# Selective scan: one scan per state group, in place, started from the last states, with a new order of a step

## The chip, the cores and the metric

The program runs on one core of one Trainium2 chip. The metric is device microseconds of one execution; below, "us" is microseconds. Engines are named as in the profile: PE (matrix products), DVE (vector), ACT (activations), POOL (the general engine), SP (issues nearly all DMAs).

## What is computed

Four layers, each added to its input `x` of 8 images of 64 x 64 positions and 96 channels, after a group norm: two selective scans (layers 0 and 2), a chunked scan (layer 1), and a layer that widens, squares and narrows the image (layer 3). The change touches layers 0 and 2 only. Each of these projects the input to 192 channels, runs a 3 x 3 convolution and a SiLU, reads the 4096 positions in four directions (rows, columns, and both backwards), and scans each direction with 16 states a channel. Cut to what matters:

```python
delta = jax.nn.softplus(delta + delta_bias[None, :, None])

def step(h, inp):
    ut, dt, bt, ct = inp
    dA = jnp.exp(dt[..., None] * A4)                  # 4 directions, 192 channels, 16 states
    dBu = (dt * ut)[..., None] * bt[:, :, None, :]
    h = h * dA + dBu
    y = jnp.einsum('bkdn,bkn->bkd', h, ct)
    return (h, y)
...
return y + u * D[None, :, None]
```

The four directions are then added up, normalised, gated and projected back. All is in fp32.

## The kernel before

`tile_vision_stack` loops over the 8 images and, for each, over the layers. `selective_scan` (called 16 times) works one layer. Its convolution comes first, partly on DVE and partly on PE. Then come 32 **steps**: four directions `k`, each in eight pieces `c` of 512 positions. Directions 2 and 3 are scanned from the end, with reversed views of the same tiles. A step has six **units** `n`, each 32 of the 192 channels. In a unit, partition 32 j + c holds state j of a group for channel c, so 16 states are four **groups** of four: a unit is a tile of 128 partitions and 4 x 512 elements.

The work of a unit `t` (counted over all steps) is spread over the engines:

- `spread` (L821): PE repeats delta times u of 32 channels over 128 partitions, to the PSUM tile `pu`. Its pool `p_misc` has one buffer.
- `with_b` (L828): the product of that with B, to the tile `db`. Units 2 and 5 run on POOL, with a copy `du2` that came through DRAM; the other four on DVE.
- `decays` (L840): ACT computes exp(A delta) in PSUM. There are two tiles `da`, each for two groups.
- `scan` (L854): DVE, h = h da + db along the row. One instruction covers two groups in one row of 1026. Each group has 513 places: the additional one holds a decay of zero and, in `db`, the state with which the group starts. `enter` (L811) copies these states on ACT from `states`, three units ahead.
- `leave` (L871): ACT keeps the last column of h as the state for the next piece; POOL multiplies h by C in place.
- `total_y` (L885): PE sums over the states of three units, on top of the `y` so far, into the PSUM tile `py`; ACT copies it to `y`. It is done twice a step, after units 2 and 5.

`prepare` (L720) is a generator that makes the inputs of a step, and `prepare_part` runs it on to its next `yield`: a projection on PE, its copy on ACT, a second projection, its copy with the DMAs that write B and C to DRAM and bring B back to 128 partitions, softplus on ACT (which changes the activation table and back), the DMAs of delta, those of `dx` for the first three units and of C, `du` = delta times u on POOL with its trip through DRAM, and last `dx` for the other three units. Both projections use `py`'s buffer (pool `p_y`, one buffer).

`Beside` (L619) runs the last layer of the image before, in pieces: `begin` issues a piece's matrix products, `end` its copy on ACT. Up to four pieces fall in a step. The first image has none.

What sets the order is the program: inside `tc.manual_schedule()` each engine, and SP as the queue of DMAs, works its instructions in the order in which the Python code issues them, and waits for semaphores where its inputs or buffers are not ready. The order is written in the loop over `t` near the end of `selective_scan`.

Of the kernel before, what the change touches and what calls it, by code (L numbers as in the profile page):

```python
# [9 lines left out]
F32 = mybir.dt.float32  # L10
AF = mybir.ActivationFunctionType
ALU = mybir.AluOpType
PSUM = bass.MemoryType.PSUM
# [9 lines left out]
LC = 512  # L23
NCH = L // LC
SEG = LC + 1
NCG = 6
NSG = 4
# [40 lines left out]
def tile_vision_stack(  # L68
# [20 lines left out]
    nc = tc.nc  # L89
# [24 lines left out]
    zero = wp.tile([128, NSG], F32, name="zero")  # L114
# [565 lines left out]
    def selective_scan(w, wdt, dgw, a, d, u, y, beside):  # L680
# [23 lines left out]
        with (  # L704
# [3 lines left out]
            tc.tile_pool(name="scan", bufs=3) as gp,  # L708
            tc.tile_pool(name="state", bufs=2) as stp,
            tc.tile_pool(name="beside", bufs=1) as bp,  # L710
            tc.tile_pool(name="p_misc", bufs=1, space=PSUM) as pmp,
            tc.tile_pool(name="p_y", bufs=1, space=PSUM) as pyp,
            tc.tile_pool(name="p_da", bufs=1, space=PSUM) as pap,
# [6 lines left out]
            def prepare(i):  # L720
# [10 lines left out]
                pv = pyp.tile([128, LC], F32, name="pv", tag="py")  # L731
# [9 lines left out]
                pv = pyp.tile([128, LC], F32, name="pv", tag="py")  # L741
# [50 lines left out]
                m["du"] = du  # L792
                dud = dp.tile([32, 2, LC], F32, name="dud")
                nc.sync.dma_start(dud, du[64:96])
                m["du2"] = du2 = tp.tile([128, 2, LC], F32, name="du2")
# [5 lines left out]
            def groups(t):  # L801

                return t[:, 1:].rearrange("p (g s) -> p g s", s=SEG)[:, :, :LC]

            def places(t, n, rev):

                return t[:, rev : n * SEG + rev].rearrange("p (g s) -> p g s", s=SEG)[
                    :, :, SEG - 1 if rev else 0
                ]

            def enter(t):  # L811

                i, n = t // units, t % units
                k, c = steps[i]
                first = c == (0 if k < 2 else NCH - 1)
                db = gp.tile([128, NSG * SEG + 1], F32, name="db")
                src = zero if first else states[i - 1][:, NSG * n : NSG * n + NSG]
                nc.scalar.copy(places(db, NSG, int(k >= 2)), src)
                made[i]["db", n] = db

            def spread(t):  # L821

                m, n = made[t // units], t % units
                rows = slice(32 * (n % 3), 32 * (n % 3) + 32)
                m["pu"] = pu = pmp.tile([128, LC], F32, name="pu", tag="misc")
                nc.tensor.matmul(pu, sel[rows, :], m["du"][rows, n // 3, :], start=True, stop=True)  # L826

            def with_b(t):  # L828

                m, n = made[t // units], t % units  # L830
                pool = n % 3 == 2
                (nc.gpsimd if pool else nc.vector).tensor_mul(  # L832
                    groups(m["db", n]),
                    (m["du2"][:, n // 3, :] if pool else m["pu"])
                    .unsqueeze(1)
                    .to_broadcast([128, NSG, LC]),
                    m["b"],
                )

            def decays(t, p):  # L840

                i, n = t // units, t % units
                k, _ = steps[i]
                dst = das[p][:, 1:].rearrange("p (g s) -> p g s", s=SEG)
                for g in range(2):
                    gs = 2 * p + g
                    nc.scalar.activation(  # L847
                        dst[:, g, :LC],
                        made[i]["dx"][n // 3][:, n % 3, :],
                        AF.Exp,  # L850
                        scale=av4[:, k, n, gs : gs + 1],
                    )

            def scan(t, p):  # L854
                i, n = t // units, t % units
                k, _ = steps[i]
                rev = int(k >= 2)
                way = slice(None, None, -1) if rev else slice(None)
                at = slice(2 * p * SEG + rev, 2 * (p + 1) * SEG + rev)
                if p == 0:  # L860
                    made[i]["h", n] = gp.tile([128, NSG * SEG + 1], F32, name="h", bufs=5)
                nc.vector.tensor_tensor_scan(  # L862
                    made[i]["h", n][:, at][:, way],
                    das[p][:, rev : 2 * SEG + rev][:, way],
                    made[i]["db", n][:, at][:, way],
                    0.0,
                    ALU.mult,
                    ALU.add,
                )

            def leave(t, more):  # L871

                i, n = t // units, t % units
                k, _ = steps[i]
                h = groups(made[i]["h", n])
                if n == 0:
                    states[i] = stp.tile([128, NCG * NSG], F32, name="state")
                nc.scalar.copy(  # L878
                    states[i][:, NSG * n : NSG * n + NSG], h[:, :, 0 if k >= 2 else LC - 1]
                )  # L880
                if more:
                    prepare_part(i + 1)
                nc.gpsimd.tensor_mul(h, h, made[i]["c"])  # L883

            def total_y(i, hf):  # L885
# [11 lines left out]
                hs = [groups(made[i].pop(("h", 3 * hf + q))) for q in range(3)]  # L897
# [14 lines left out]
            def prepare_part(i):  # L912
                if i < len(steps):
                    if i not in going:
                        going[i] = prepare(i)
                    next(going[i], None)
# [5 lines left out]
            das = [pap.tile([128, 2 * SEG + 1], F32, name=f"da{p}") for p in range(2)]  # L922
# [16 lines left out]
            for da in das:  # L939
                for at in range(3):  # L940
                    nc.vector.memset(da[:, at * SEG : at * SEG + 1], 0.0)
# [4 lines left out]
            for _ in range(2):  # L946
                prepare_part(0)
            conv_half(6, 0, pyp, "py")
            for t in range(3):
                enter(t)  # L950
            decays(0, 0)
            decays(0, 1)
# [12 lines left out]
            spread(0)  # L965
            for _ in range(3):
                prepare_part(1)
            conv(w, y, u, (40, 48), 0)
            with_b(0)
            other = Beside(ops)  # L970
            for t in range(total + 2):
                n, i = t % units, t // units
                ahead = t + 1 < total
                quota = (i + 1) * len(ops) // len(steps) - i * len(ops) // len(steps)
                if n == 2 and quota > 1:
                    other.begin(pyp, "py")
                if n in (0, 3) and ahead:
                    spread(t + 1)
                elif n == 1 and t + 2 < total:
                    spread(t + 2)  # L980
                if n == 0 and i > 0:
                    sums = total_y(i - 1, 1)
                elif n == 3:
                    sums = total_y(i, 0)
                elif n == 4:
                    if quota > 3:
                        other.begin(pmp, "misc")
                    if t + 2 < total:
                        spread(t + 2)
                    prepare_part(i + 2)  # L990
                elif n == 5:
                    prepare_part(i + 2)
                if t < total:
                    scan(t, 0)
                    if n % 3 == 0 and t + 2 < total:
                        with_b(t + 2)
                if ahead:
                    decays(t + 1, 0)
                if n == 1:
                    if t > 1:  # L1000
                        nc.scalar.copy(*sums)
                    if t < total:
                        other.begin(pyp, "py")
                elif n == 2:
                    other.end()
                    if quota > 2:
                        other.begin(pyp, "py")
                elif n == 3:
                    other.end()
                elif n == 4:  # L1010
                    nc.scalar.copy(*sums)  # L1011
                    other.end()
                if t < total:
                    scan(t, 1)
                    leave(t, n == 3)
                if t + 3 < total:
                    enter(t + 3)
                if ahead:
                    decays(t + 1, 1)
                    if (n + 1) % 3 != 2:  # L1020
                        with_b(t + 1)
                if n in (1, 2):
                    other.end()
                    if n == 2 and quota > 4:
                        other.begin(pyp, "py")
                if n in (4, 5):
                    prepare_part(i + 2)
                if n in (0, 1, 5):
                    prepare_part(i + 1)
# [815 lines left out]
```

## Time and profile before

| | us |
|---|---|
| median of three runs | 26687.65 (26685.59 to 26688.1) |
| the profiled execution | 26693.06 |
| its span, first to last instruction | 26691.2 |
| one selective scan, first to last scan instruction, first image | 1159.2, 1159.3 |
| the same, later images (fourteen) | 1186.3 to 1207.1, mean 1195.5 |
| all sixteen | 19055 |

The profile page gives the busy time of each engine, a row per group of equal instructions (line, engine, operation, output <- inputs, shapes, count; then busy us, mean ns of one; then the idle time of the engine before them, and what ended it), and the waits. "L862" is a line of the kernel. A timeline lists the instructions of an engine by start and length, with equal neighbours merged. Since neighbours on an engine may overlap a little, the price of an instruction in a row is read from start to start. The table's last three lines come from the first and last scan of each layer.

### The profile page before, as it was taken

Reading aid. Unit: us, or ns where it says so; the run is one execution under the profiler, and the core shown is the slowest. Engines: PE = TensorE matmul, PEld = TensorE weight load, DVE = VectorE, ACT = ScalarE, POOL = GpSimd, SP = SyncE. Lnnn points to the kernel's source line nnn. Section 1 sums busy time; section 2 is a strip of 40 time slices with the busy share of each in tenths; the row PEclk is TensorE's granted clock in tenths of the full one; section 3 lists DMA queues with packets and bytes.
Section 4 is the critical chain, followed back from the end, with each engine's and each line's share of the span. In section 5 each row is a group of like instructions: output and inputs, shape, how many; then the busy total and the mean of one; then the engine's idle time right before and its main releaser. Section 6 shows DMA issues by size and latency. Waiting matters only on the chain. (4 is left out here: it accounts for less than half of the span.)

```text
span 26691.2 us, 282273 instructions
## 1 busy us (share of the span) xinstructions
PE 21984.9 (82%) x90981; PEld 8484.0 (32%) x90981; DVE 23982.3 (90%) x16689; ACT 16407.9 (61%) x29921; POOL 21235.6 (80%) x7928
## 2 busy tenths in 40 slices
PE   6796788888888878888888887888888888788888
PEld 2151222422224222242223422234222342223424
DVE  9989999898998989889898898988989889898896
ACT  5656566565665656556565565655656556565564
POOL 8949898497975979759797697976979769796694
PEclk7787777877778777787778877788777887778878
DMA  5515454154541545425453254532545325453352
GB/s 125 122 35 129 120 129 109 41 132 123 131 107 47 131 123 132 102 50 133 123 132 97 58 132 123 133 90 62 132 123 132 85 68 133 123 133 78 75 132 68
DMA packets 1678115, 2836.59 MB, mean 106 GB/s; under 512 B 434473, under 2 KB 477769, under 8 KB 1672033
## 3 DMA queue, kind: packets, MB, share of 16 engines
q1 hardware_dynamic: 1660000, 2812.23, 43.3%
q8 instruction: 731, 11.98, 0.2%
q10 hardware_dynamic: 16640, 6.29, 0.1%
q14 instruction: 744, 6.09, 0.1%
HBM read 2390.02 MB, written 427.49 MB: 106 GB/s over the span
## 5 line engine op out<-in xcount | busy, mean ns | idle before, releaser
L862 DVE TENSOR_TENSOR_SCAN h<-da,db 128x1026 f32<-128x1026 f32 x6144 | 13745.7, 2281 | 744.8 <-ACT da L847 378.5
L883 POOL TENSOR_TENSOR h<-h,c 128x2048 f32<-128x2048 f32 x3072 | 12743.1, 4172 | 968.2 <-ACT state L878 528.3
L900 PE MATMUL py<-h,cst 128*32 128x512 f32 x24576 | 5344.6, 749 | 473.0 <-POOL h L883 472.6
L847 ACT ACTIVATE da<-dx,a0s 128x512 f32<-128x512 f32 x6144 | 4239.6, 690 | 1548.8 <-DVE h L862 1373.0
L847 ACT ACTIVATE da<-dx,a2s 128x512 f32<-128x512 f32 x6144 | 4239.2, 690 | 1546.5 <-DVE h L862 1375.0
L832 POOL TENSOR_TENSOR db<-du,b 128x2048 f32<-128x2048 f32 x1024 | 4661.3, 4552 | 306.7 <-DMA du<-dud 226.5
L832 DVE TENSOR_TENSOR db<-pu,b 128x2048 f32<-128x2048 f32 x2048 | 4643.3, 2267 | 141.6 <-PE pu L826 138.2
L826 PE MATMUL pu<-du,cst 32*128 32x512 f32 x4096 | 2940.8, 805 | 1455.7 <-DVE db L832 927.4
L900 PEld LDWEIGHTS py<-h,cst 128*32 128x32 f32 x24576 | 1217.5, 133 | 4997.2 <-issue 3829.7
L826 PEld LDWEIGHTS pu<-du,cst 32*128 32x128 f32 x4096 | 735.2, 223 | 3145.9 <-DVE db L832 1580.8
L743 PE MATMUL pv<-u,wk 96*128 96x512 f32 x2048 | 1290.5, 762 | 388.1 <-ACT raw L738 388.1
L506 PE MATMUL ps<-s,w3as 96*128 96x512 f32 x1344 | 1069.4, 888 | 641.7 <-ACT sf L513 258.9
L1349 ACT ACTIVATE sg<-sg 128x768 f32<-128x768 f32 x1024 | 819.6, 800 | 862.2 <-PE sg L1333 862.2
L890 PE MATMUL py<-y,cst 96*96 96x512 f32 x1536 | 1306.1, 946 | 9.0 <-ACT y L1011 5.7
L733 PE MATMUL pv<-u,wk 96*96 96x512 f32 x2048 | 1200.9, 716 | 59.6 <-DVE u L281 27.4
L1303 POOL TENSOR_TENSOR ce<-ec,cr 112x512 f32<-112x512 f32 x256 | 521.5, 2037 | 754.9 <-ACT ec L1301 736.6
L1381 DVE TENSOR_TENSOR wt<-wt,cbm 128x768 f32<-128x768 f32 x1024 | 990.6, 1001 | 128.9 <-ACT wt L1350 128.1
L878 ACT COPY state<-h 128x4 f32<-128x4 f32 x3072 | 588.6, 192 | 796.5 <-DVE h L862 788.2
L526 PE MATMUL ps<-w3bs,sf 128*128 128x96 f32 x5376 | 1071.5, 356 | 0.0
L314 POOL TENSOR_SCALAR xn<-xs,sb 96x512 f32<-96x512 f32 x192 | 204.8, 1069 | 997.9 <-PE pz L319 440.8
L526 PEld LDWEIGHTS ps<-w3bs,sf 128*128 128x128 f32 x5376 | 992.9, 270 | 0.0
L738 ACT COPY raw<-pv 96x512 f32<-96x512 f32 x512 | 297.6, 581 | 970.1 <-PE pv L733 943.5
(238 smaller groups left out, 29900.9 us busy)
## 6 DMA issues: line engine op xcount, KB each, us to landing
dx<-dd SPq DMA_DIRECT2D x4096, 192.0 KB
b<-bcd SPq DMA_DIRECT2D x2048, 256.0 KB
c<-bcd SPq DMA_DIRECT2D x2048, 256.0 KB
du<-dud SPq DMA_DIRECT2D x2048, 128.0 KB
dd<-raw SPq DMA_DIRECT2D x1024, 192.0 KB
dud<-du SPq DMA_DIRECT2D x512, 128.0 KB
xd<-xs SPq DMA_DIRECT2D x256, 192.0 KB
cr<-bcd SPq DMA_DIRECT2D x1536, 32.0 KB
```

The source lines that it names most:

```text
L506: nc.tensor.matmul(ps, w3as[:, m * 128 : (m + 1) * 128], live["x2"], start=True, stop=True)
L526: nc.tensor.matmul(po, live["f"][m][:, at : at + 128], w2q[:, m, :], start=False, stop=(m == 2),)
L733: nc.tensor.matmul(pv[:DM], weights[k][:, hi, 128:], uv[hi], start=(hi == 0), stop=(hi == 1))
L743: nc.tensor.matmul(pv, weights[k][:, hi, :128], uv[hi], start=(hi == 0), stop=(hi == 1))
L826: nc.tensor.matmul(pu, sel[rows, :], m["du"][rows, n // 3, :], start=True, stop=True)
L832: (nc.gpsimd if pool else nc.vector).tensor_mul(groups(m["db", n]), (m["du2"][:, n // 3, :] if pool else m["pu"]) .unsqueeze(1) .to_broadc ...
L847: nc.scalar.activation(dst[:, g, :LC], made[i]["dx"][n // 3][:, n % 3, :], AF.Exp, scale=av4[:, k, n, gs : gs + 1],)
L862: nc.vector.tensor_tensor_scan(made[i]["h", n][:, at][:, way], das[p][:, rev : 2 * SEG + rev][:, way], made[i]["db", n][:, at][:, way], 0. ...
L883: nc.gpsimd.tensor_mul(h, h, made[i]["c"])
L890: nc.tensor.matmul(py, skip[:, hf, :] if k == 0 else ident[:DM, :DM], near((u if k == 0 else y)[:, hf, :], wh, c * LC, LC), start=True, st ...
L900: nc.tensor.matmul(turn_back(py[32 * q : 32 * q + 32, :], wh, LC), red, cut(hs[q][:, g, :], wh), start=False, stop=(g == NSG - 1),)
L1381: nc.vector.tensor_mul(it["wt"], it["wt"], m["cbm"][:, j : j + 1, :].to_broadcast([128, RK, Q]),)
```

## The change

Nine edits, all in `selective_scan`:

- The scan works one group of 512 at a time, 24 instructions a step in place of 12. Its input and output are the same tile `h`: `with_b` writes there, and the scan overwrites it. The first value of a group is no place of the row any more but an operand, a column of `states` (or of `zero` at a direction's first piece).
- The additional places, `enter`, `groups`, `places` and the memsets of the separators are gone. The pool `scan` has 8 tiles `h` (before, 3 `db` and 5 `h`). `room` takes a unit's tile ahead of its writer, in the order of units.
- `da` is four PSUM tiles, one a group, and each is refilled right after its scan.
- `p_misc` has two buffers, so that two spreads can be ahead.
- A new PSUM pool `p_side` with one buffer serves the projections of `prepare` and the pieces of `Beside`, which leave `p_y` to `total_y`.
- `prepare` has two more `yield`s: the product `du`, its way to DRAM and its way back are three parts.
- The loop follows a table `plan`: for each unit, words issued ahead of the scans and after each of the four scans. `a`: room; `b`: product with B; `s`: spread; `p`: begin a piece; `e`: end it; `y`: sum of y; `c`: its copy; `r`: a part of `prepare`. The number is how many units (or steps, for `r`) ahead, and for `p` which piece of the step.
- The products with B on DVE stand between a unit's second and third scan, for the next unit (before: behind the unit's last scan, right ahead of the scan that reads them). On POOL, `du` now comes before the product with C of unit 2 (before: of unit 3).
- The sum of y of units 3 to 5 stands at the next step's start behind a spread and a piece, its copy in unit 2 (before: unit 1). That of units 0 to 2 stands in unit 4 (before: unit 3), its copy at the end of unit 5 (before: unit 4).

```diff
-            tc.tile_pool(name="scan", bufs=3) as gp,
+            tc.tile_pool(name="scan", bufs=8) as gp,
...
-            tc.tile_pool(name="p_misc", bufs=1, space=PSUM) as pmp,
+            tc.tile_pool(name="p_misc", bufs=2, space=PSUM) as pmp,
             tc.tile_pool(name="p_y", bufs=1, space=PSUM) as pyp,
+            tc.tile_pool(name="p_side", bufs=1, space=PSUM) as psp,
...
-                pv = pyp.tile([128, LC], F32, name="pv", tag="py")
+                pv = psp.tile([128, LC], F32, name="pv", tag="ps")
...
                 m["du"] = du
+                yield
                 dud = dp.tile([32, 2, LC], F32, name="dud")
                 nc.sync.dma_start(dud, du[64:96])
+                yield
                 m["du2"] = du2 = tp.tile([128, 2, LC], F32, name="du2")
...
-                m["pu"] = pu = pmp.tile([128, LC], F32, name="pu", tag="misc")
+                m["pu", n] = pu = pmp.tile([128, LC], F32, name="pu", tag="misc")
...
+            def room(t):
+
+                m, n = made[t // units], t % units
+                if ("h", n) not in m:
+                    m["h", n] = gp.tile([128, NSG, LC], F32, name="h")
+                return m["h", n]
...
+            def decay(t, g):
 
                 i, n = t // units, t % units
                 k, _ = steps[i]
+                nc.scalar.activation(
+                    das[g],
+                    made[i]["dx"][n // 3][:, n % 3, :],
+                    AF.Exp,
+                    scale=av4[:, k, n, g : g + 1],
+                )
+
+            def scan(t, g):
+                i, n = t // units, t % units
+                k, c = steps[i]
+                way = slice(None, None, -1) if k >= 2 else slice(None)
+                first = c == (0 if k < 2 else NCH - 1)
+                at = NSG * n + g
+                h = made[i]["h", n][:, g, :][:, way]
+                nc.vector.tensor_tensor_scan(
+                    h,
+                    das[g][:, way],
+                    h,
+                    zero[:, g : g + 1] if first else states[i - 1][:, at : at + 1],
+                    ALU.mult,
+                    ALU.add,
+                )
...
-            das = [pap.tile([128, 2 * SEG + 1], F32, name=f"da{p}") for p in range(2)]
+            das = [pap.tile([128, LC], F32, name=f"da{g}") for g in range(NSG)]
...
+            plan = (
+                ("a1 b2 s3 p1 y", "", "b1 s4", "", "e p2"),
+                ("", "", "", "", "r1 e p3"),
+                ("r1", "", "b1 c e p4", "", ""),
+                ("a1 b2 s3 s4", "e", "b1 r2", "", "r2"),
+                ("r1 y r2", "", "r1", "", ""),
+                ("r1", "", "b1", "", "c r2"),
+            )
...
+                for word in plan[n][0].split():
+                    act(word, t, quota)
+                for g in range(NSG):
+                    scan(t, g)
+                    if g == NSG - 1:
+                        leave(t, n == 2)
+                    if t + 1 < total:
+                        decay(t + 1, g)
+                    for word in plan[n][1 + g].split():
+                        act(word, t, quota)
+            nc.scalar.copy(*total_y(len(steps) - 1, 1))
```

`leave`'s second argument says that a part of `prepare` (the product `du`) goes on POOL's queue ahead of the unit's product with C.

## The prediction

> **What bounds the kernel now.** I read the page's busy shares first, then a table of windows, then the costliest groups, the waits, and last the timeline of one step, engine by engine. Here are the shares, and one window of 100 us in the first image's selective scan and one in the second's (columns: PE, PEld, DVE, ACT, POOL busy, granted clock, DMA share, GB/s).
>
> ```profile
> PE 21984.9 (82%) x90981; PEld 8484.0 (32%) x90981; DVE 23982.3 (90%) x16689; ACT 16407.9 (61%) x29921; POOL 21235.6 (80%) x7928
> ...
> 600.00:700.00 100.00, 70.16 (x176) 20.21 (x176) 98.15 (x45) 62.05 (x120) 100.00 (x26) 0.72 0.53 130
> 4000.00:4100.00 100.00, 82.93 (x234) 26.66 (x233) 95.27 (x44) 66.11 (x126) 96.27 (x25) 0.74 0.52 123
> ```
>
> In this stage DVE and POOL are both full: a gain on one alone ends at the other. From the second image on, the previous image's last layer runs beside the scan, and DVE falls to 95%. The groups:
>
> ```profile
> L862 DVE TENSOR_TENSOR_SCAN h<-da,db 128x1026 f32<-128x1026 f32 x6144 | 13745.7, 2281 | 744.8 <-ACT da L847 378.5
> L883 POOL TENSOR_TENSOR h<-h,c 128x2048 f32<-128x2048 f32 x3072 | 12743.1, 4172 | 968.2 <-ACT state L878 528.3
> ...
> L832 POOL TENSOR_TENSOR db<-du,b 128x2048 f32<-128x2048 f32 x1024 | 4661.3, 4552 | 306.7 <-DMA du<-dud 226.5
> L832 DVE TENSOR_TENSOR db<-pu,b 128x2048 f32<-128x2048 f32 x2048 | 4643.3, 2267 | 141.6 <-PE pu L826 138.2
> ```
>
> One step (512 positions of one direction, six units) is 12 scans, 4 DVE products and 2 POOL products with B, 6 POOL products with C. DVE in the timeline (start, length; merged runs have a count):
>
> ```profile
> 600.03 4.48 DVE L862 TENSOR_TENSOR_SCAN h<-da,db 128x1026 f32<-128x1026 f32 x2 [0.34 <-ACT da L847]
> 604.42 2.27 DVE L832 TENSOR_TENSOR db<-pu,b 128x2048 f32<-128x2048 f32 x1
> 606.79 4.48 DVE L862 TENSOR_TENSOR_SCAN h<-da,db 128x1026 f32<-128x1026 f32 x2
> ...
> 613.56 8.85 DVE L862 TENSOR_TENSOR_SCAN h<-da,db 128x1026 f32<-128x1026 f32 x4
> 622.32 2.26 DVE L832 TENSOR_TENSOR db<-pu,b 128x2048 f32<-128x2048 f32 x1
> ...
> 636.28 4.48 DVE L862 TENSOR_TENSOR_SCAN h<-da,db 128x1026 f32<-128x1026 f32 x2 [0.34 <-ACT da L847]
> ```
>
> A step lasts 636.28 - 600.03 = 36.25 us. Four scans in a row take 622.32 - 613.56 = 8.76, so one is 2.19 from start to start, and 2.185 when the one before overlaps it. A scan behind the product that makes its input starts 0.10 after that product ends (604.42 + 2.27 = 606.69, then 606.79); a scan behind a scan starts 0.08 before its end. That wait costs 0.21 with the longer first scan, and comes four times a step. Sum: 12 x 2.185 + 4 x 2.18 + 4 x 0.21 + 0.45 for the wait on da = 36.23.
>
> POOL, and the block on ACT that causes the 0.34:
>
> ```profile
> 598.50 12.43 POOL L883 TENSOR_TENSOR h<-h,c 128x2048 f32<-128x2048 f32 x3
> 610.87 4.55 POOL L832 TENSOR_TENSOR db<-du,b 128x2048 f32<-128x2048 f32 x1
> 615.35 2.89 POOL L785 TENSOR_TENSOR du<-raw,u 96x1024 f32<-96x1024 f32 x1
> 618.16 12.46 POOL L883 TENSOR_TENSOR h<-h,c 128x2048 f32<-128x2048 f32 x3
> ```
>
> ```profile
> 4028.71 1.28 ACT L767 ACT_TABLE_LOAD   x1
> 4030.01 1.33 ACT L767 ACTIVATE raw<-raw,w0s 96x512 f32<-96x512 f32 x2
> 4031.36 1.28 ACT L847 ACT_TABLE_LOAD   x1
> ```
>
> By starts, POOL has 6 x 4.12 + 2 x 4.48 + 2.81 = 36.5 us of work a step where k is odd, and 36.0 where it is even (du is 0.5 shorter): 36.25 again.
>
> From first to last scan a layer takes 1159.2 us in the first image (twice) and 1195.5 on average in the other fourteen; together 19,055 us. So the other images lose 36.3 / 32 = 1.13 us a step, mostly to decays that stand behind ACT's copy of a projection not yet made (us in total, times, longest):
>
> ```profile
> ACT raw L738 <- PE pv L733: 943.5, 491, 5.4
> ```
>
> **The change, part by part.** *Scans.* 12 of 1026 become 24 of 512. An element costs (2.281 - 0.14) / 1026 = 2.08 ns (0.14 is what the 2048-wide product has above 1.04 ns an element), so the old scan is 2.137 of elements and 0.048 of the rest, start to start. Half of it, with an immediate first value, would be 1.067 + 0.048 = 1.115. But the first value is now a column in SBUF, and no scan of the trace has that. The nearest rows are other DVE instructions with and without such a column, in merged runs:
>
> ```profile
> 1485.92 1.11 DVE L1447 SCALAR_TENSOR_TENSOR y<-u,d,py 96x128 f32<-96x128 f32 x4
> 1490.41 1.82 DVE L1381 TENSOR_TENSOR wt<-wt,cbm 128x768 f32<-128x768 f32 x2
> ```
>
> With a column: (1.11 - 0.334) / 3 = 0.259, less 0.133 of elements, is 0.126. Without: 1.82 - 0.951 = 0.869, less 0.800, is 0.069. The column costs 0.057, and I take 1.115 + 0.057 = 1.172. Ends: 1.115 (it costs nothing; a gain is excluded, it is one more read) and 1.215 (twice that).
>
> [...] The trace has the row first: 0.048 us between chained scans. [...]
>
> *Products with B on DVE.* Same four of 2.18, but issued between scans two scans ahead of their reader, so the four waits of 0.21 go; 0.84 a step. If the reader waited after all, that is the price.
>
> *Decays.* ACT's 24 exponentials stay (690 ns each). Each has its own PSUM tile and is refilled right after its scan, needed three scans later (3.5 us, 5.7 across a product). The softplus block, 3.95 us, falls behind unit 1's last decay; unit 2 lasts 4 x 1.172 + 2.18 = 6.87, so its end is met with some 1.5 us to spare and the 0.45 goes.
>
> *Enter copies and separators.* 3072 copies of 0.19 us on ACT (idle for 38% of a window) and 96 tiny memsets: nothing on the path.
>
> *Sum on DVE*: 24 x 1.172 + 4 x 2.18 = 36.85 a step, 0.6 above the 36.25 of the first image, 0.5 below the others' 37.36.
>
> *Spreads, y, pieces (PE, ACT).* The spread matmuls go up to two ahead into two PSUM buffers; projections and the pieces beside have a buffer of their own, so they no longer queue for the one that y uses. y of the second half is put behind a spread and a piece, its copy moves from unit 1 to unit 2, the first half's to unit 5: later than POOL's products need (below). PE's waits on db (927 us) lose their cause. Cover: PE is 83% busy beside the last layer, with 17% left.
>
> *POOL.* Units start at 0, 6.9, 11.6, 18.4, 25.3, 30.0. Its queue: product 5 of the step before to 4.2, B of unit 2 to 8.7, products 0 and 1 to 17.0, du (moved ahead of product 2) to 19.5, product 2 to 23.7, B of unit 5 to 28.2, products 3, 4 to 36.4. B of unit 2 is 2.9 us early, B of unit 5 1.8. Behind du stand product 2 and that B; du needs softplus, done at about 15. POOL's 36.0 to 36.5 is now just under DVE's 36.85.
>
> *SP.* The same DMAs. du's trip through DRAM is issued in three parts, and the repeat of dx for units 3 to 5 passes b's copies; dx lands sooner, b later, but b is read a step later. Worst case: b late by a few us, hidden by some 30.
>
> *State pools.* 8 tiles of h instead of 3 db and 5 h: a unit reuses the tile of eight units before, summed long ago. Nothing.
>
> *What is late next.* ACT's raw copy in unit 3 waits for a projection behind two spreads that wait for du (19.5) on PE; the row above gives such waits 1.9 us on average, 5.4 at most. With four pieces most are absorbed; I leave 0.15 a step in the fourteen layers (between 0 and the 1.13 of now, nearer to 0 because a piece is due only 3.5 us later).
>
> A layer: 32 x 36.85 - 0.6 (the last step lacks a product, the first has a start; before: 1159.2 against 32 x 36.25) = 1178.6, and 4.8 more in fourteen. Together 16 x 1178.6 + 14 x 4.8 = 18,925, that is 130 under 19,055. The profiled run is 26,693.1 (span 26,691.2 and 1.9 around it), 5.4 above the median of three; 26,687.65 - 130 = **26,558 us**, 0.5% faster. Each 10 ns on a scan is 24 x 32 x 16 x 0.01 = 123 us, so sign and size hang on one unseen price.
>
> **Rivals.** *The column is free.* Then DVE needs 35.5 and POOL rules with 36.25 on average and some start: about 1167 a layer, 380 less, 26,305. For it: the state is 1 element. Against: every row with a column has it dearer.
>
> *The column is dear, and it gets slower.* At 1.215 a step is 37.9, a layer 1212, the sum 19,452, +397: 27,085. It decides from 1.183 upwards. For it: L1400, 96 wide (0.10), lets the next instruction start 0.23 after it (1490.18 to 1490.41), 0.13 of the rest, and a scan carries a value from element to element besides. Against: the other rows with a column.
>
> *The wait moves.* The 1.13 a step stays in fourteen layers, since PE is as busy and in order: 14 x 32 x 0.98 = 440 more than forecast, 27,000. It decides from 0.44 us a step. For: ACT's copies still wait for PE behind y and spreads. Against: more slack at every decay.
>
> *A port is shared.* The two rows of DVE with a column, min/median/max:
>
> ```profile
> L1447 DVE SCALAR_TENSOR_TENSOR y<-u,d,py x512: 329/334/341, 1473.3 to 24647.1; 96x128 f32<-96x128 f32 x171
> L1400 DVE SCALAR_TENSOR_TENSOR state<-state,ec,own x960: 317/320/4296, 1475.0 to 24938.7; 112x96 f32<-112x96 f32 x192
> ```
>
> L1400 reads two tensors from SBUF and is held up to a whole POOL product; L1447 reads one from SBUF, one from PSUM and a column, and never is. The new scan is of the second kind, as the old. If the column counted as a second tensor, scans would wait for POOL, over 30,000 us. [...]
>
> **How the numbers follow.** Forecast 0.45 (26,450 to 26,660); column free 0.13; dear 0.20; wait moves 0.19; port 0.03. Under 0.2% (53 us) is about what this kernel's measurement can't tell from nothing. Faster: 0.40 of the forecast and 0.13; same: 0.05 of it and 0.06 of the next two; slower: the rest, 0.36. The range goes from the free column to the dear one, 26,290 to 27,090.
>
> **What would show it.** Scan 128x512 at about 1.25 us long and 1.17 from start to start (1.20 long: free); no 0.10 gap behind a product; DVE at 98 to 99% of a window in all images; POOL just under full; the wait of DVE for da near nothing. Wrong if scans vary in length beside POOL, if DVE waits for POOL's B of unit 5, or if ACT's raw copy still waits 900 us and DVE with it.

## The result, and the profile after

The changed kernel takes 27267.37 us (median of four runs, 27249.25 to 27281.73), the kernel before, beside it, 26686.62. The ratio is 1.0219, with a 95% interval of 1.0201 to 1.0236: 2.2% slower. The forecast was 26,558, and the time lies above the price of every rival but the shared port (over 30,000).

The profiled execution took 27281.73, its span is 27279.9. Its page, first the busy shares of the engines:

```profile
PE 21616.5 (79%) x90981; PEld 8670.6 (32%) x90981; DVE 24755.6 (91%) x22737; ACT 15768.8 (58%) x26849; POOL 22282.6 (82%) x7928
```

The table of windows of the changed kernel, in the first and in the second image's scan (columns: PE, PEld, DVE, ACT, POOL busy, granted clock, DMA share, GB/s):

```profile
600.00:700.00 100.00, 64.57 (x196) 16.31 (x195) 95.32 (x73) 56.06 (x97) 100.00 (x24) 0.74 0.50 120
4000.00:4100.00 100.00, 76.54 (x238) 24.18 (x241) 95.77 (x74) 58.49 (x105) 100.00 (x25) 0.75 0.51 126
```

Before, DVE stood at 98% and 95%, POOL at 100% and 96%. Now POOL is full in both and DVE is not full in either: POOL alone sets the step. The costliest groups of the changed kernel (shapes; busy us, mean ns of one | idle before, and what ended it):

```profile
L870 POOL TENSOR_TENSOR h<-h,c 128x2048 f32<-128x2048 f32 x3072 | 13888.9, 4561 | 502.8 <-ACT state L865 254.3
L849 DVE TENSOR_TENSOR_SCAN h<-da,state,h 128x512 f32<-128x512 f32 x10752 | 12855.2, 1259 | 609.2 <-POOL h L823 505.7
...
L823 POOL TENSOR_TENSOR h<-du,b 128x2048 f32<-128x2048 f32 x1024 | 4682.0, 4572 | 304.9 <-DMA du<-dud 206.8
L823 DVE TENSOR_TENSOR h<-pu,b 128x2048 f32<-128x2048 f32 x2048 | 4632.8, 2262 | 0.0
```

The first row is the one to stop at. The product with C is the same instruction, with the same shapes and the same count, as before; there it took 4172 ns, now 4561. That is 3072 x 0.389 = 1,195 us more of POOL by these means. The scan has the length that was forecast (1.26 against "about 1.25"). The timeline of DVE in the changed kernel, over one step:

```profile
604.98 2.46 DVE L849 TENSOR_TENSOR_SCAN h<-da,state,h 128x512 f32<-128x512 f32 x2 [1.57 <-POOL h L823]
607.35 2.26 DVE L823 TENSOR_TENSOR h<-pu,b 128x2048 f32<-128x2048 f32 x1
609.54 4.79 DVE L849 TENSOR_TENSOR_SCAN h<-da,state,h 128x512 f32<-128x512 f32 x4
614.25 2.26 DVE L823 TENSOR_TENSOR h<-pu,b 128x2048 f32<-128x2048 f32 x1
616.43 9.49 DVE L849 TENSOR_TENSOR_SCAN h<-da,state,h 128x512 f32<-128x512 f32 x8
```

The old gap of 0.10 behind a product is gone (607.35 + 2.26 = 609.61, and the scan starts at 609.54). In its place DVE waits once, 1.57 us, for POOL's product with B. POOL in the same stretch has no pause:

```profile
600.42 4.52 POOL L823 TENSOR_TENSOR h<-du,b 128x2048 f32<-128x2048 f32 x1
604.91 13.48 POOL L870 TENSOR_TENSOR h<-h,c 128x2048 f32<-128x2048 f32 x3
618.36 4.54 POOL L823 TENSOR_TENSOR h<-du,b 128x2048 f32<-128x2048 f32 x1
622.87 8.97 POOL L870 TENSOR_TENSOR h<-h,c 128x2048 f32<-128x2048 f32 x2
631.81 2.85 POOL L786 TENSOR_TENSOR du<-raw,u 96x1024 f32<-96x1024 f32 x1
634.62 4.49 POOL L870 TENSOR_TENSOR h<-h,c 128x2048 f32<-128x2048 f32 x1
639.08 4.52 POOL L823 TENSOR_TENSOR h<-du,b 128x2048 f32<-128x2048 f32 x1
```

From one product with B to the same one of the next step, 639.08 - 600.42 = 38.66 us; with the shorter du of even k the mean is 38.4. A step's work of DVE, without the wait, is 37.1. The waits of the changed kernel's DVE (us in total, times, longest) say the same for the whole run:

```profile
DVE h L849 <- POOL h L823: 572.1, 437, 1.7
...
DVE h L849 <- ACT da L835: 104.9, 36, 5.2
```

A layer now lasts 1223.1 in the first image and 1228.1 on average in the others; all sixteen 19,639, which is 584 more than the 19,055 of before, and the run lost 581. So the whole loss lies in these steps. POOL's 1,195 us show only by half, because in the fourteen later layers POOL was not full before (96%) and a step already took 37.36 (1195.5 / 32): there it went to 38.38, in the first image from 36.23 to 38.22. What is left to find is why POOL's product is slower.

### The profile page after: what moved, and what is told of

Read it like the earlier page. It is cut to its first block, busy times and chain, and to the rows that moved or that the text cites. A ratio compares the mean times of both kernels' runs of the same rounds, so it can differ in the third digit from the quotient of the medians.

```text
span 27279.9 us, 284141 instructions
## 1 busy us (share of the span) xinstructions
PE 21616.5 (79%) x90981; PEld 8670.6 (32%) x90981; DVE 24755.6 (91%) x22737; ACT 15768.8 (58%) x26849; POOL 22282.6 (82%) x7928
## 5 line engine op out<-in xcount | busy, mean ns | idle before, releaser
L870 POOL TENSOR_TENSOR h<-h,c 128x2048 f32<-128x2048 f32 x3072 | 13888.9, 4561 | 502.8 <-ACT state L865 254.3
L849 DVE TENSOR_TENSOR_SCAN h<-da,state,h 128x512 f32<-128x512 f32 x10752 | 12855.2, 1259 | 609.2 <-POOL h L823 505.7
L887 PE MATMUL py<-h,cst 128*32 128x512 f32 x24576 | 4935.3, 708 | 217.6 <-POOL h L870 215.2
L823 POOL TENSOR_TENSOR h<-du,b 128x2048 f32<-128x2048 f32 x1024 | 4682.0, 4572 | 304.9 <-DMA du<-dud 206.8
L823 DVE TENSOR_TENSOR h<-pu,b 128x2048 f32<-128x2048 f32 x2048 | 4632.8, 2262 | 0.0
L809 PE MATMUL pu<-du,cst 32*128 32x512 f32 x4096 | 2560.8, 892 | 1709.8 <-POOL du L786 782.4
L734 PE MATMUL pv<-u,wk 96*96 96x512 f32 x2048 | 1878.3, 1072 | 43.4 <-DMA wk<-wdt 21.8
L849 DVE TENSOR_TENSOR_SCAN h<-da,zero,h 128x512 f32<-128x512 f32 x1536 | 1843.5, 1260 | 72.2 <-POOL h L823 66.4
L744 PE MATMUL pv<-u,wk 96*128 96x512 f32 x2048 | 1070.6, 647 | 11.1 <-ACT raw L739 11.1
L522 PE MATMUL ps<-w,s 96*128 96x96 f32 x1792 | 512.5, 380 | 696.9 <-ACT raw L748 334.7
L739 ACT COPY raw<-pv 96x512 f32<-96x512 f32 x512 | 297.6, 581 | 1316.6 <-issue 1212.0
```

Source lines behind the costliest of these rows:

```text
L734: nc.tensor.matmul(pv[:DM], weights[k][:, hi, 128:], uv[hi], start=(hi == 0), stop=(hi == 1))
L744: nc.tensor.matmul(pv, weights[k][:, hi, :128], uv[hi], start=(hi == 0), stop=(hi == 1))
L823: (nc.gpsimd if pool else nc.vector).tensor_mul(h, (m["du2"][:, n // 3, :] if pool else m.pop(("pu", n))) .unsqueeze(1) .to_broadcast([128 ...
L849: nc.vector.tensor_tensor_scan(h, das[g][:, way], h, zero[:, g : g + 1] if first else states[i - 1][:, at : at + 1], ALU.mult, ALU.add,)
L887: nc.tensor.matmul(turn_back(py[32 * q : 32 * q + 32, :], wh, LC), red, cut(hs[q][:, g, :], wh), start=False, stop=(g == NSG - 1),)
```

## Experiments

Theories of the loss: L, how the product's two inputs lie in SBUF (h has no additional places any more, so h and C are both plain 4 x 512); P, the column that each scan now reads disturbs POOL; O, the order: POOL's products run beside other work than before; and a fourth, that DVE would be slower anyway, with POOL as its companion only.

### h in rows of 513 again

```diff
-                    m["h", n] = gp.tile([128, NSG, LC], F32, name="h")
+                    m["h", n] = gp.tile([128, NSG * SEG + 1], F32, name="h")[:, 1:].rearrange("p (g s) -> p g s", s=SEG)[:, :, :LC]
```

The changed kernel, with a group's 512 elements at place 1 + 513 g as before; the additional places stay unused.

> The changed kernel with one thing put back: the tiles h have rows of 513 from element 1 on, as before the change; scan, order and buffers stay those of the change. After the change POOL's product with C takes 4.56 us in place of 4.17, and 6 of these a step make POOL the bound. Theory L (layout: the product is dearer because h and C now lie alike in memory): the product is back at 4.15 to 4.20, POOL has 36.0 to 36.5 a step, DVE rules with 36.9, 16 layers of about 1180: 26,500 to 26,650 us. Theory P (the first value's column, read by DVE, disturbs POOL): the product stays at 4.5 and the time at 27,270. Theory O (the order: POOL's products run beside other work than before): stays as well.

Measured: 26677.41 us, 1.0002 of the kernel before beside it (0.9992 to 1.0011). The groups of this run:

```profile
L849 DVE TENSOR_TENSOR_SCAN h<-da,state,h 128x512 f32<-128x512 f32 x10752 | 12855.7, 1260 | 133.9 <-ACT da L835 107.8
L870 POOL TENSOR_TENSOR h<-h,c 128x2048 f32<-128x2048 f32 x3072 | 12768.0, 4171 | 993.4 <-ACT state L865 817.8 <-DMA b<-bcd 110.6 <-DMA sc<-x1d 54.7
```

And its windows:

```profile
600.00:700.00 100.00, 59.45 (x172) 15.23 (x172) 99.86 (x76) 61.14 (x104) 98.79 (x25) 0.72 0.51 131
4000.00:4100.00 100.00, 80.30 (x254) 30.67 (x250) 99.85 (x77) 63.85 (x112) 97.35 (x26) 0.74 0.53 135
```

The product is back at 4.17, DVE's wait for POOL is gone from the row, and DVE is full in both windows. This one line gives back the whole loss, with every column and the new order still there: that speaks for L and against P and O, and DVE's own slowness is not what lost 2.2%. But it gives no gain either, and is 27 us above the expectation's upper end. That is DVE's own sum, and the timeline of DVE in this run shows by how much it was off:

```profile
603.68 9.50 DVE L849 TENSOR_TENSOR_SCAN h<-da,state,h 128x512 f32<-128x512 f32 x8
613.10 2.26 DVE L823 TENSOR_TENSOR h<-pu,b 128x2048 f32<-128x2048 f32 x1
...
622.17 9.67 DVE L849 TENSOR_TENSOR_SCAN h<-da,state,h 128x512 f32<-128x512 f32 x8
631.76 2.27 DVE L823 TENSOR_TENSOR h<-pu,b 128x2048 f32<-128x2048 f32 x1
```

Eight scans take 613.10 - 603.68 = 9.42, so 1.178 each, the first behind a product included; the other eight take 9.59. What holds these up is seen on ACT and PE in the same run:

```profile
611.67 1.28 ACT L768 ACT_TABLE_LOAD   x1
612.96 1.33 ACT L768 ACTIVATE raw<-raw,w0s 96x512 f32<-96x512 f32 x2
...
628.12 0.58 ACT L739 COPY raw<-pv 96x512 f32<-96x512 f32 x1 [2.67 <-POOL h L823]
628.60 1.91 ACT L835 ACTIVATE da<-dx,a0s 128x512 f32<-128x512 f32 x3
...
624.31 3.73 PE L734 MATMUL pv<-u,wk 96*96 96x512 f32 x4
```

It isn't the softplus block (L768), which is long over by then; the four scans right behind it (615.28 to 619.99) take no more than 4.71. It is ACT's raw copy (L739): it reads the projection that PE ends at 628.04 (L734), though the view names POOL's B as what ended its wait. By the single records the first decay behind the copy ends at 629.29, and its scan, the seventh of the eight, starts at 629.39, where it was due at 629.24. In the first image's layers 30 of the 32 steps have this gap (the last two prepare nothing). A step is 9.42 + 9.59 + 2 x 4.71 of scans (the two other stretches have four each) and 4 x 2.18 of products: 37.15, where the forecast had 36.85.

### The first value an immediate zero

```diff
-                    zero[:, g : g + 1] if first else states[i - 1][:, at : at + 1],
+                    0.0,
```

> The changed kernel with an immediate 0.0 as each scan's first value: the states of the last piece are not carried over, so the values of later pieces lack them; nothing else differs. Theory L: POOL's product stays at 4.5 and rules, so the time stays within 0.3% of 27,270, while the scan gets shorter by the price of the column (0.057 us by the prediction: 1.12 from start to start). Theory P: the product is back at 4.17, POOL rules with 36.3, about 26,330. Theory O: as L.

Measured: 27241.92, ratio 1.0215 (1.02 to 1.023). The groups of this run:

```profile
L849 DVE TENSOR_TENSOR_SCAN h<-da,h 128x512 f32<-128x512 f32 x12288 | 13999.8, 1200 | 1316.3 <-ACT da L835 1011.0 <-POOL h L823 266.3 <-POOL h L870 2.1
L870 POOL TENSOR_TENSOR h<-h,c 128x2048 f32<-128x2048 f32 x3072 | 13885.2, 4561 | 465.8 <-ACT state L865 280.7 <-DMA b<-bcd 184.7
```

Without any column POOL's product is as slow as with it, to the nanosecond: P falls again. The scan is 0.06 shorter, and the time stays, since POOL rules.

### C moved in the kernel before, and in the changed one

```diff
-                    t = pool.tile([128, NSG, LC], F32, name=name)
+                    t = pool.tile([128, NSG, LC] if name == "b" else [128, NSG * SEG + 1], F32, name=name)
+                    if name == "c":
+                        t = t[:, 1:].rearrange("p (g s) -> p g s", s=SEG)[:, :, :LC]
```

The tile `dg`, which comes from the same buffers, gets the same shape. In the kernel before, whose h is in rows of 513, this makes C lie as h does. In the changed kernel, whose h is plain, it makes them differ.

> The kernel before with the tiles of C in the layout that h has there, rows of 513 from element 1 on; so h and C lie alike again, both odd. Theory L in the form 'the two inputs lie alike': the product goes from 4.17 to 4.5, 2.2 us a step on POOL, about +1,000 us less what POOL had idle: 27,300 to 27,600. Theory L in the form 'a tile whose rows start at a multiple of 2 KB is dear': it stays at 4.17 or falls, 26,690. Theories P and O: 26,690, since neither column nor order is there.

Measured: 27298.58, ratio 1.0236 (1.0221 to 1.0251), 1.4 us under the expected range. The groups of this run:

```profile
L885 POOL TENSOR_TENSOR h<-h,c 128x2048 f32<-128x2048 f32 x3072 | 13832.6, 4544 | 516.4 <-ACT state L880 498.1 <-issue 11.8 <-POOL h L885 5.5
L864 DVE TENSOR_TENSOR_SCAN h<-da,db 128x1026 f32<-128x1026 f32 x6144 | 13777.5, 2282 | 1343.5 <-ACT da L849 863.2 <-PE py L902 180.4 <-POOL db L834 91.3
```

With nothing else of the change, neither its order nor its column, the kernel before becomes as slow as the changed one. Rows of 513 are not fast in themselves: here both inputs have them.

> The changed kernel with the tiles of C in rows of 513 from element 1 on, h contiguous as the change has it: the inputs lie unlike each other, with the roles exchanged against the kernel before. 'Inputs lie alike': the product falls to 4.17 and the time to 26,500 to 26,650, as with h moved. 'h's own rows': the product stays at 4.5, 27,270. Theories P and O: 27,270.

Measured: 26685.95, ratio 1.0007 (0.9997 to 1.0016), 36 us above the expectation's end, for the reason that the first experiment gave. The group in this run:

```profile
L872 POOL TENSOR_TENSOR h<-h,c 128x2048 f32<-128x2048 f32 x3072 | 12761.8, 4169 | 1000.7 <-ACT state L867 795.3 <-DMA b<-bcd 135.9 <-DMA sc<-x1d 55.1
```

It does not matter which input is moved (4171 ns with h, 4169 with C), as long as the two lie differently. That leaves: differently in what sense?

### The shift, unit by unit

```diff
-                    m["h", n] = gp.tile([128, NSG, LC], F32, name="h")
+                    off = (0, 1, 2, 4, 8, 16)[n]
+                    h = gp.tile([128, NSG * LC + 16], F32, name="h")[:, off : off + NSG * LC]
+                    m["h", n] = h.rearrange("p (g s) -> p g s", s=LC)
...
```

The product also has a line of its own for each unit, so that one run measures six shifts of h against C, in elements of 4 bytes. A second run has shifts (2, 3, 5, 6, 7, 10).

> The changed kernel with h of unit 0, 1, 2, 3, 4, 5 moved by 0, 1, 2, 4, 8, 16 elements (0, 4, 8, 16, 32, 64 bytes) in a tile of 2064; rows stay 512 apart, and POOL's product has a line of its own for each unit. Theory L, inputs alike modulo a small line: unit 0 at 4.5 us, units 1, 2, 3 at 4.17, and where the line's length is reached (32 or 64 bytes) it is back at 4.5. If only odd places help (rows of 513 rather than the shift), all stay at 4.5. If any shift helps, all but unit 0 are at 4.17. Time between 26,690 and 27,270.

Measured: 26926.53 in one run, and the medians of 512 instructions each: shift 0: 4526 ns, 1: 4532, 2: 3813, 4: 4560, 8: 4520, 16: 4526. Only the 2 is cheap, and it is cheaper than anything before; none of the three outcomes that I had expected came. Minimum, median and maximum of the units with shift 1 and 2 in this run:

```profile
L876 POOL TENSOR_TENSOR h<-h,c x512: 4490/4532/4837, 127.9 to 26511.4; 128x2048 f32<-128x2048 f32 x171
L878 POOL TENSOR_TENSOR h<-h,c x512: 3797/3813/4131, 134.8 to 26516.4; 128x2048 f32<-128x2048 f32 x171
```

> As the run with six shifts, now with h of unit 0 to 5 moved by 2, 3, 5, 6, 7, 10 elements. Rows of 513 give the four groups shifts of 1, 2, 3 and 4, and a product of 4.17 us; with 4.53 for a shift of 1, 3.81 for 2 and 4.56 for 4 the shift of 3 must give (4 x 4.17 - 4.53 - 3.81 - 4.56) = 3.78. Theory M (the place modulo 4 elements, 16 bytes, decides; 0 and 1 dear, 2 and 3 cheap): 2, 3, 6, 7, 10 at 3.8 us and 5 at 4.5. Rival (only 2 is special): 3.8 for 2 alone or for 2, 6 and 10, the others at 4.5.

Measured: 26651.96 in one run; shift 2: 3812, 3: 3812, 5: 4517, 6: 3809, 7: 3808, 10: 3811. The units with shift 3, 5 and 7 in this run:

```profile
L876 POOL TENSOR_TENSOR h<-h,c x512: 3797/3812/3841, 127.8 to 26239.8; 128x2048 f32<-128x2048 f32 x171
L878 POOL TENSOR_TENSOR h<-h,c x512: 4498/4517/4555, 134.7 to 26246.3; 128x2048 f32<-128x2048 f32 x171
L882 POOL TENSOR_TENSOR h<-h,c x512: 3797/3808/3842, 147.4 to 26259.0; 128x2048 f32<-128x2048 f32 x171
```

In these eleven shifts only the remainder by 4 elements (16 bytes) counts: 0 and 1 cost 4.53, 2 and 3 cost 3.81. It isn't the unit: each of the six was dear in one of the two runs and cheap in the other. This also explains the old figure: with rows of 513 the four groups of one product have the shifts 1, 2, 3 and 4, and (2 x 4.53 + 2 x 3.81) / 4 = 4.17, as measured.

### Both products of POOL at a shift of 2

```diff
-                    t = pool.tile([128, NSG, LC], F32, name=name)
+                    at_ = 2 if name == "b" else 0
+                    t = pool.tile([128, NSG * LC + at_], F32, name=name)[:, at_:]
+                    t = t.rearrange("p (g s) -> p g s", s=LC)
...
-                    m["h", n] = gp.tile([128, NSG, LC], F32, name="h")
+                    h = gp.tile([128, NSG * LC + 2], F32, name="h")[:, 2:]
+                    m["h", n] = h.rearrange("p (g s) -> p g s", s=LC)
```

> The changed kernel with h and B moved by 2 elements in their tiles, C and du2 as they are. Theory M: POOL's products with C fall to 3.81 and with B to about 3.85; POOL has some 33.3 us a step. DVE rules with 37.17 as with rows of 513: 26,600 to 26,700 us, no more than there, since POOL is far below.

Measured: 26653.69, ratio 0.9999 (0.9989 to 1.0008). The table of windows of this run:

```profile
600.00:700.00 100.00, 62.34 (x171) 15.84 (x172) 99.86 (x76) 60.36 (x102) 90.78 (x26) 0.71 0.54 131
4000.00:4100.00 100.00, 80.71 (x241) 27.51 (x242) 99.78 (x76) 63.96 (x113) 86.55 (x25) 0.71 0.58 138
```

```profile
L826 POOL TENSOR_TENSOR h<-du,b 128x2048 f32<-128x2048 f32 x1024 | 3907.4, 3816 | 308.4 <-DMA du<-dud 250.1 <-DMA dx<-dd 58.3
```

POOL's products take 3811 (C) and 3816 ns (B, the row above), POOL is idle for a tenth of the time, and nothing is won: DVE is at 99.8%, and its step of 37.15 is the bound. In the kernel before, too, DVE is the limit (again with the tile `dg` in the same shape):

```diff
-                    t = pool.tile([128, NSG, LC], F32, name=name)
+                    t = pool.tile([128, NSG, LC] if name == "b" else [128, NSG * SEG + 3], F32, name=name)
+                    if name == "c":
+                        t = t[:, 3 : 3 + NSG * SEG].rearrange("p (g s) -> p g s", s=SEG)[:, :, :LC]
...
```

> The kernel before with C in rows of 513 from element 3, two places from h, which has them from element 1. Theory M: POOL's product with C falls from 4.17 to 3.81, POOL has 34.1 us a step. If DVE's 36.25 was the bound of the kernel before as much as POOL's, the first image's layers stay at 1,155 to 1,159 and the time at 26,550 to 26,690; if POOL was the one that ruled, they fall towards 1,120 and the time below 26,300.

Measured: 26701.02, ratio 1.001 (1.0 to 1.0019), 11 us above the expectation's end. The product with C in this run:

```profile
L885 POOL TENSOR_TENSOR h<-h,c 128x2048 f32<-128x2048 f32 x3072 | 11685.3, 3816 | 2042.6 <-issue 1020.5 <-ACT state L880 914.7 <-POOL h L885 99.4
```

It takes 3816 ns, and a layer of the first image 1157.1 in place of 1159.2. So before, DVE set the step and POOL stood right behind it.

### What the column costs in time

The first experiment's layout together with the immediate zero of the second (the states are not carried on here either).

> The changed kernel with h in rows of 513 and an immediate 0.0 as each scan's first value (the last piece's states are not carried over). With h in rows of 513 DVE rules with 37.17 us a step. Theory C (the column of the first value costs 0.06 us a scan, as it does in the other DVE rows): 24 x 0.06 = 1.44 us a step go, DVE has 35.7, POOL rules with about 36.3: 16 layers of about 1,167, 26,250 to 26,350 us. Rival (the scan's price is that of splitting, not of the column): within 0.3% of 26,680.

Measured: 26230.01, ratio 0.9836 (0.9821 to 0.9851), 20 us below the expectation; scan, product and a window of this run:

```profile
L849 DVE TENSOR_TENSOR_SCAN h<-da,h 128x512 f32<-128x512 f32 x12288 | 13945.0, 1197 | 429.3 <-ACT da L835 286.7 <-POOL h L823 140.8
L870 POOL TENSOR_TENSOR h<-h,c 128x2048 f32<-128x2048 f32 x3072 | 12825.8, 4219 | 571.1 <-ACT state L865 353.0 <-DMA b<-bcd 213.8 <-DMA sr<-xd 1.4
...
600.00:700.00 100.00, 64.73 (x182) 17.25 (x182) 97.81 (x77) 61.08 (x106) 100.00 (x26) 0.74 0.56 133
```

The column is 0.063 of a scan's length here, 0.060 in the second experiment. It is worth 26677.41 - 26230.01 = 447 us of the clock; 12288 x 0.063 = 774 would be, had POOL, which is full here, not become the bound on the way. So I tried to take the column off DVE: the kernel with both products at a shift of 2, the scan with an immediate zero, and the first value added by ACT, as decay times state plus input, into the group's first element:

```diff
...
+                nc.scalar.activation(
+                    h,
+                    das[g][:, f : f + 1],
+                    AF.Identity,
+                    scale=states[i - 1][:, at : at + 1],
+                    bias=h,
+                )
...
```

> The same, and the first value is no operand of the scan any more: ACT adds da x state to the first element of each group (24 instructions of about 0.35 us a step, where ACT has some 14 us idle), and the scan begins with an immediate 0.0. Full computation. If the column's 0.06 us a scan is what DVE pays, DVE has 35.7 and nothing is above it: 32 x 35.7 a layer, 1,142, with some waits 25,850 to 26,150, faster than both kernels. Rival (the added ACT work comes late, and DVE waits for it): 26,300 or more.

Measured: 27148.86, ratio 1.018 (1.0163 to 1.0197). The waits of DVE in this run:

```profile
DVE h L850 <- ACT h L868: 1253.6, 1250, 4.1
```

The scan is down to 1200 ns, but DVE now waits for these small activations, up to 24 a step and 347 ns each: the rival named in the expectation. The time is 495 us above that of the same layout with the column.

### The product's new place, in the kernel before

```diff
+                    if ahead and (n + 1) % 3 != 2:
+                        with_b(t + 1)
...
-                    if (n + 1) % 3 != 2:
-                        with_b(t + 1)
```

The product with B on DVE stands between a unit's two scans, and nothing else of the change is done. A second kernel has B in rows of 513 besides.

> The kernel before with one thing of the change: DVE's product with B for the next unit stands between a unit's two scans, not behind them, so the next scan need not wait for it. Theory D (the four waits of 0.21 us are DVE's loss): DVE has 35.4 us a step, but POOL still 36.25, so the first image's layers stay at 1,155 to 1,160, the others gain at most some: 26,450 to 26,690. Rival (the wait goes over to the spread on PE, which has 2.2 us less): 26,700 to 27,000.

Measured: 28421.17, ratio 1.0659 (1.0641 to 1.0676), far outside. The waits of DVE in this run:

```profile
DVE db L832 <- PE pu L826: 1317.0, 637, 4.4
DVE h L862 <- ACT da L847: 969.0, 399, 7.4
```

The product comes half a unit earlier, and the spread that it reads does not: `p_misc` has one buffer. I had underpriced that. The changed kernel, with two buffers and its new order, has no idle time at all before these products (0.0 in the row of L823 above). Which of the two gives that was not tried apart.

> The same, and the tiles of B in rows of 513 from element 1 on, unlike du2, with which POOL multiplies them. Theory L for the other POOL product: it falls from 4.55 to about 4.17, POOL has 35.5 us a step, and since DVE has 35.4 the step falls to 35.6 to 36.2: 26,250 to 26,500, faster than both kernels. Rival (the 4.55 is due to the input that is repeated over the four groups, not to how the two lie): it stays at 4.55 and the time at that of the run without it.

Measured: 28379.25, ratio 1.0639 (1.0623 to 1.0655), far outside as well. POOL's product with B fell from 4542 to 4183 ns, so the rule holds for this product too; the time did not follow, since the waits for the spread rule here: DVE is idle for 1,280 us before its products, 1,318 in the run without rows of 513.

## Why the prediction was wrong

- **The step that failed: "*State pools.* 8 tiles of h instead of 3 db and 5 h: … Nothing."** I looked at when the tiles come free, not at where their elements lie. The change takes h out of its rows of 513, and by that alone each product with C goes from 4.17 to 4.56. In the sum for POOL, "products 0 and 1" and the rest were taken at the 4.12 from start to start of the old row; they measured 4.48. Six times 0.36 is 2.2 us a step: POOL's "36.0 to 36.5 … now just under DVE's 36.85" became 38.4. The cover that I named, DVE's longer step, ended 1.2 us short.
- **What came in its place.** "B of unit 5 1.8" us early turned into a wait of DVE for POOL's B, 572 us in all. The prediction names it as a sign of being wrong; none of the rivals has a price for it. Rival 1 has POOL ruling, but with the old 36.25.
- **The rest of the miss.** Forecast 18,925 for the sixteen layers; the changed kernel has 19,639, and with h in rows of 513 it is 19,102. So of 714 us the layout makes 537. The other 177 is DVE's sum. A layer of the first image has 1186.9 in place of 1178.6 (16 x 8.3 = 133), from some 0.3 a step: 0.17 behind ACT's late raw copy, 0.13 over the scans (1.178 for 1.172). The raw copy is the one that "What is late next" names; I left 0.15 a step for it in the fourteen later layers and nothing in the first image, where the steps pay it as well. "The 0.45 goes" was right: in these layers no scan waits for the softplus block any more. The fourteen later layers have 8.0 more than that in place of the 4.8 that I left for late decays (14 x 3.2 = 45). With the layout right, the change would have been no gain and no loss.
- **Right, but in part by luck: the price of the scan.** The column costs 0.060 (forecast 0.057, from two quite different instructions), the scan 1.18 from start to start (1.172). Luck is in the choice of the row without a column, as long as an element counts 1.04 ns, a figure that the prediction takes from no row: by L832, with 2.18 - 2048 x 0.00104 = 0.05 of the rest in place of 0.069, the same working gives 0.076 for the column and 1.19 for the scan, beyond the 1.183 at which the forecast turns to slower. The products of 2048 (L832) and of 96 elements (L1398, 254 ns) in the kernel before show (2267 - 254) / (2048 - 96) = 1.03 in its place; with that the two rows have 0.07 and 0.08 of the rest, and the same working gives 1.18 and 1.17, both below 1.183. Two sums are off: "1.215 (twice that)" should be 1.115 + 2 x 0.057 = 1.229, which puts the range's upper end at some 27,260, still below the time measured; and an element costs 2.087 by the working shown, not 2.08, some 30 us in all. The scans without a column (2281 ns before, 1200 in the second experiment) show (2281 - 1200) / (1026 - 512) = 2.10 in place of either.
- **Right: the price of 12 more scans.** Without a column a scan is 1.197 long, less the 0.08 of overlap 1.117 from start to start. Two of them take 2.234, one scan of 1026 took 2.185: 0.05 more, and 0.6 a step for 12, as the row's 0.048 had it (12 x 0.048 = 0.58).
- **Right: the waits that go.** The four gaps behind a product went, and the later images lose 0.25 a step on average (8.0 / 32) in place of 1.13: with h in rows of 513 a layer 0 lasts 1186.9 in the first image and 1188.2 in the later ones. ACT is still idle for 1,317 us before its raw copy (in the changed kernel and with h in rows of 513 alike), which I had named as a danger; but the waits of DVE for decays that its table of waits shows are down to 112.7 with h in rows of 513, from 378.5 before. So most of it is absorbed, as forecast; the 0.17 a step above comes on top. A layer 2 of the later images loses 14 us, most of it by the trace in its last four steps; I didn't test why.
- **Right: POOL does not hold the scans.** The 10,752 scans with a column of `states` take 1247 to 1285 ns in the changed kernel, where POOL is full in both windows. None is held as L1400 was (median 0.32): in the kernel before, one of these started at 1571.06 and took 4.29, until 0.12 after a chain of POOL instructions (1571.29 to 1575.23). The "over 30,000 us" of that rival is worked out from no row, and no run shows scans that wait so.
- **Rival 1, as a price.** "The column is free" was put at 26,305 with POOL as the bound; with rows of 513 and no column it measured 26,230.
- **Between the scans.** The stretches between the layers' scans are 70 us shorter with h in rows of 513 than in the changed kernel. POOL's last products, which end 1.4 to 2.3 us sooner behind each layer's last scan, are some 30 of it. The other 40 I haven't followed. So the tie with the kernel before has two parts: 47 us more in the sixteen layers (19,102 against 19,055) and 66 less between them.

No version here that carries the states on beats the kernel before. Rows of 513 or a shift of 2 make the change a tie. The next gain has to come off DVE's 37.15, and the one try at that put the wait on ACT.

## What to carry to other kernels

When a change alters the shape or the start of a tile, every instruction that reads it gets its price anew, also those that the diff doesn't touch: compare where the two inputs of a product lie, not only how long they are. Where two engines are as close as these (POOL 36.0 to 36.5, DVE 36.85 us a step in the forecast), add up both queues with the new layout before trusting that one covers the other. A padding that looks like a mere by-product of an algorithm can carry speed: here 0.39 us of each product with C, and 590 us of the run.

## What the runs showed of the hardware

- A POOL product of two fp32 inputs of 128 x 2048 took 3.81 us where h lay 2 or 3 elements past C, modulo 4, and 4.53 where it lay 0 or 1 past. It held for eleven different shifts, and the same two prices appear with C moved by 2 (3816, in the kernel before) and for the product with B (3816 against 4572). Where the result lay did not count: the product with B of the kernel before wrote to rows of 513 and, with its two inputs lying alike, took the dear 4552. The step between the two is 19%. What makes the period of 16 bytes, no run shows.
- A first value read from an SBUF column costs a scan 0.060 us, with POOL full (1259 against 1200 ns) and with POOL idle for a tenth of the time (1259 against 1200, both products at a shift of 2).
- With h in rows of 513, a scan that had to wait for ACT's decay started 0.10 us after that decay's end (629.29 to 629.39). The merged timeline shows no idle time there; by the single records there is a gap of 0.07, and the overlap of 0.08 with the scan before it is lost. Together with a somewhat longer scan that is the 0.17.
